# Pairwise bilinear products in FP32 parts: whole-pair PSUM tiles for VectorE, and a different place for the two-part weight loads

## The chip, the cores and the metric

The kernel runs on one NeuronCore of a Trainium2 chip. The metric is the device time of one execution in microseconds (us). The time before is 750.67 us, the median of three runs (748.7 to 752.8). One further execution was taken by the hardware profiler; all profile lines come from it.

## The reference

There are 32 fields of 128 numbers for each of 1024 rows of the batch, and one 128x128 matrix for each of the 496 pairs of fields i < j. Each pair's result is field i times its matrix, multiplied element by element with field j.

```python
FIELD_SIZE, EMBED_SIZE = 32, 128
_pairs = np.array(list(itertools.combinations(range(FIELD_SIZE), 2)), dtype=np.int32)   # 496 pairs
v_i = inputs[:, I_IDX, :]            # inputs: (1024, 32, 128) fp32
v_j = inputs[:, J_IDX, :]
transformed = jnp.einsum('bpd,ped->bpe', v_i, W)      # W: (496, 128, 128) fp32
return transformed * v_j             # (1024, 496, 128) fp32, 260 MB
```

## The kernel before, in words

**Layout.** Everything is held transposed: the 128 embedding positions lie on the partitions and the 1024 batch rows along them. The host only permutes inputs and outputs. Pairs are walked from i = 30 down to i = 0, and for each i over j = i+1 to 31, so a later field has more pairs (31 - i). A pair q is worked in two halves h of 512 batch rows; the loop counter u = 2q + h counts halves, 992 in all.

**Arithmetic.** The first 15 pairs (five fields, `NATIVE`) use plain FP32 matmuls (L209). All others split operands into parts that TensorE multiplies in its faster FP32R form. A matrix W becomes wh (ScalarE, L127), wl and wd (GpSimd, L128 to L130), two pairs at a time (`split_w`; 241 such chunks). A field x becomes xh (ScalarE, L142), xl (GpSimd, L143 and L144) and xd, half by half (`split_x`). For 16 fields xd is made on VectorE (L265), for the ten last ones on GpSimd (L148).

**One half.** `first(u)` takes a PSUM buffer, adds up the products wh·xh and wl·xl (L212), and ScalarE multiplies the sum in place by 1 + 2^-12 (L213). `second(u)`, called three halves later (`LAG = 3`), adds the third product wd·xd (L221). Then VectorE multiplies the PSUM buffer with field j into an output tile (L227). A PSUM buffer is 128x512, one bank; there are eight.

**Output.** Four pairs share an output tile of 2 MB, which is stored by one DMA from ScalarE's queue (L258) once all of it is written. There are seven such tiles at first. Four of them lie where groups of x fields are loaded later (L108, at the pairs of `XAT`), so that from pair 293 on only three are left.

**Weights.** W arrives in blocks of eight pairs, 512 KB, into three slots (`rpool`, `WB = 3`). Most blocks come by one DMA on SyncE's queue (L118). From block 12 on, every second one (`WAPART`) comes in two parts: 112 of the 128 rows by a DMA that GpSimd issues (L102), the other 16 by SyncE (L103). `back` notes that a few pairs later a tiny DMA of GpSimd's follows (`move_on`, L99). When each load is issued stands in a table `w_at`: for block c it is mostly pair 8c - 17. Near the end field 0 is loaded into one of the three W slots (`load_x(0)`).

**Order.** The order of instructions on each engine is that of the program text (`manual_schedule`); each engine works through its own list and waits where it needs another's result. W and x splits stand in `todo` with the earliest pair and the due pair; one of them is issued for each pair, the one due first. The GpSimd list is therefore a sequence of W chunks, with x halves put in wherever no chunk is ready.

Of the kernel before, what the change touches and what calls it, by code (L numbers as in the profile page):

```python
# [7 lines left out]
F32 = mybir.dt.float32  # L8
F32R = mybir.dt.float32r
ALU = mybir.AluOpType  # L10

P = 128
NF = 32
NQ = NF * (NF - 1) // 2
BT = 1024
HB = 512
WC = 2
WL = 8
OG = 4
EPS = 2.0**-12  # L20
NATIVE = 5
SHARED = 16
XDLAG = 10
LAG = 3
WB = 3
WLEAD = 12
XAFTER = 54
# [3 lines left out]
NE = 14  # L31
ROWS = 8 * NE
WAPART = tuple(range(12, 62, 2))
BACK = 3
XAT = (313, 219, 141, 52)
OWAIT = 20
SLAG = 2


def _pairs():  # L40
# [5 lines left out]
def kernel(  # L46
# [22 lines left out]
    nc = tc.nc  # L69
# [4 lines left out]
    spool = ctx.enter_context(tc.tile_pool(name="xs", bufs=2))  # L74
    rpool = ctx.enter_context(tc.tile_pool(name="wr", bufs=WB))
    wpool = ctx.enter_context(tc.tile_pool(name="ws", bufs=4))
    opool = ctx.enter_context(tc.tile_pool(name="o", bufs=1))
    ppool = ctx.enter_context(tc.tile_pool(name="ps", bufs=8, space=bass.MemoryType.PSUM))

    x_sb = {}  # L80

    def load_x(f, pieces=1, eng=None):
        if f == 0:

            t = rpool.tile([P, WL, P], F32, tag="w", name="x_0").rearrange("p q e -> p (q e)")
        else:
            t = xpool.tile([P, BT], F32, tag=f"x{f}", name=f"x_{f}")
        s = BT // pieces
        for k in range(pieces):
            (eng or nc.sync).dma_start(out=t[:, k * s : (k + 1) * s], in_=xt[f, :, k * s : (k + 1) * s])  # L90
        x_sb[f] = t

    w_raw = {}
# [3 lines left out]
    def move_on(k):  # L97

        nc.gpsimd.dma_start(out=mark[: 2 * k], in_=xt[0, : 2 * k, :16].rearrange("(b a) n -> a b n", a=k))  # L99

    def load_apart(dst, src):
        nc.gpsimd.dma_start(out=dst[:ROWS], in_=src[:ROWS].rearrange("(b a) m n -> a b m n", a=NE))  # L102
        nc.sync.dma_start(out=dst[ROWS:], in_=src[ROWS:])  # L103

    def load_group(k):
        t = xpool.tile([P, XG, BT], F32, tag=f"g{k}", name=f"x_g{k}")
        f = XG * k + 1
        nc.sync.dma_start(out=t, in_=xt[f : f + XG].rearrange("m d b -> (m d b)").rearrange("(d m b) -> d m b", m=XG, b=BT))  # L108
        for m in range(XG):
            x_sb[f + m] = t[:, m, :]  # L110

    def load_w(c, splits=(0, WL), eng=nc.sync):
        w_raw[c] = rpool.tile([P, WL, P], F32, tag="w", name=f"w_{c}")
        if c in WAPART:
            load_apart(w_raw[c], wt[c])
            return
        for a, b in zip(splits, splits[1:]):
            eng.dma_start(out=w_raw[c][:, a:b, :], in_=wt[c, :, a:b, :])  # L118

    w_s = {}  # L120

    def split_w(c, u):

        k = c * WC % WL
        raw = w_raw[c * WC // WL][:, k : k + WC, :].rearrange("p q e -> p (q e)")
        h, l, d = [wpool.tile([P, WC * P], F32R, tag=t, name=f"{t}_{c}") for t in ("wh", "wl", "wd")]
        nc.scalar.mul(h, raw, 1.0 - 2.0**-13)  # L127
        nc.gpsimd.tensor_tensor(l, raw, h.bitcast(F32), ALU.subtract)  # L128
        nc.gpsimd.tensor_scalar(d, h.bitcast(F32), EPS, 1.0, ALU.mult, ALU.mult)  # L129
        nc.gpsimd.tensor_tensor(d, l.bitcast(F32), d.bitcast(F32), ALU.subtract)  # L130
        w_s[c] = (h, l, d)

    x_s = {}
    later = []

    def split_x(f, a, u):
# [8 lines left out]
        if f > NF - 2 - NATIVE - SHARED:  # L145
            later.append((min(u + XDLAG, 2 * first_q[f] + LAG - 1), d, h.bitcast(F32), l.bitcast(F32)))
        else:
# [9 lines left out]
    for c in range(c0, nchunk):  # L157
        todo.append(((c - 3) * WC + 1, max(c * WC, nq0), lambda u, c=c: split_w(c, u)))
# [16 lines left out]
    w_at = {}  # L175
    for c in range(WB, -(-NQ // WL)):
        free = (c - WB + 1) * WL if (c - WB) * WL < nq0 else 0
        early = 0 if XAFTER < c <= XAFTER + WB else WLEAD - 6
        w_at[max(c * WL - 3 * WC - 5 - early, free)] = c
    x_at = XAFTER * WL - 11  # L180
    assert x_at not in w_at and len(w_at) == NQ // WL - WB

    w_q = {c: q for q, c in w_at.items()}
    back = []

    ngroup = NF // XG // 2
    group_at = {q: k for k, q in enumerate(XAT)}
# [4 lines left out]
    def out_tile(g):  # L192
        t = min((t for t in used if (g + 1) * OG <= until.get(t, NQ + OG)), key=used.get)
        used[t] = g
        pool = xpool if t in until else opool
        return pool.tile([P, OG, BT], F32, tag=t, name=f"ot_{g}")

    ctx.enter_context(tc.manual_schedule())
    po, ots, stores = {}, {}, []


    def first(u):
        q, h = divmod(u, 2)
        i, c = pairs[q][0], q // WC
        r = slice(q % WC * P, (q % WC + 1) * P)
        s = slice(h * HB, (h + 1) * HB)
        po[u] = ppool.tile([P, HB], F32, tag="po", name=f"po_{u}")
        if q < nq0:
            nc.tensor.matmul(po[u], w_raw[q // WL][:, q % WL, :], x_sb[i][:, s], start=True, stop=True)  # L209
        else:  # L210
            for t in (0, 1):
                nc.tensor.matmul(po[u], w_s[c][t][:, r], x_s[i][t][:, s], start=t == 0, stop=t == 1)  # L212
            nc.scalar.mul(po[u], po[u], 1.0 + EPS)  # L213

    def second(u):
        q, h = divmod(u, 2)
        i, j = pairs[q]
        r = slice(q % WC * P, (q % WC + 1) * P)
        s = slice(h * HB, (h + 1) * HB)
        if q >= nq0:  # L220
            nc.tensor.matmul(  # L221
                po[u], w_s[q // WC][2][:, r], x_s[i][2][:, s], start=False, stop=True, skip_group_check=True
            )
        g, k = divmod(q, OG)
        if k == 0 and h == 0:
            ots[g] = out_tile(g)
        nc.vector.tensor_tensor(ots[g][:, k, s], po.pop(u), x_sb[j][:, s], ALU.mult)  # L227
        if q >= NQ - 2:
            stores.append((u + SLAG, out[g, :, k, s], ots[g][:, k, s]))
        elif g == 0 or q >= NQ - OG:  # L230
            if h == 1:
                stores.append((u + SLAG, out[g, :, k], ots[g][:, k]))
        elif k == OG - 1 and h == 1:
            stores.append((u + SLAG, out[g], ots[g]))

    for u in range(2 * NQ + LAG + SLAG):
        q = u // 2
        if u < 2 * NQ:
            i, j = pairs[q]
            if u % 2 == 0 and j == i + 1 and XG * ngroup < i - 2 - XLEAD:  # L240
                load_x(i - 2 - XLEAD)
            first(u)
            if u == 2 * nq0:
                move_on(5)
            if u % 2 == 0 and q in group_at:
                load_group(group_at[q])
            if u % 2 == 1 and q in w_at:
                load_w(w_at[q])
                if w_at[q] in WAPART:
                    back.append(q + BACK)  # L250
            if u % 2 == 0 and q in back:
                move_on(16 - NE if q < w_q[WAPART[-1]] else 13)
            if u == 2 * x_at + 1:
                load_x(0)
        if LAG <= u < 2 * NQ + LAG:
            second(u - LAG)
        while stores and stores[0][0] <= u - LAG:
            nc.scalar.dma_start(*stores.pop(0)[1:])  # L258
        if u % 2 == 1:
            ready = [t for t in todo if t[0] <= q]  # L260
            if ready:
                ready[0][2](u)
                todo.remove(ready[0])
        while later and later[0][0] <= u:
            nc.vector.tensor_tensor(*later.pop(0)[1:], ALU.subtract)  # L265
    assert not todo and not later and not stores
# [32 lines left out]
```

## Time and profile before

| what | us |
|---|---|
| median of three runs | 750.67 |
| the profiled execution, its own time | 750.21 |
| its span, first to last instruction | 748.4 |
| PE busy (2946 matmul records) | 699.0 |
| VectorE busy | 678.0 |
| ScalarE busy | 623.9 |
| GpSimd busy | 611.5 |
| bytes moved by DMA | 310 MB, mean 414 GB/s |

The time of an execution is a little over its span, since starting and ending lie outside. In the profile PE is TensorE's matmul and PEld its weight load, DVE is VectorE, ACT ScalarE, POOL GpSimd and SP SyncE. A name such as "L213 ACT po<-po" gives the line of the kernel, the engine, and what is written from what. "Idle before" tells how long the engine stood before such an instruction and who released it. The granted TensorE clock was 0.984 of full speed.

### The profile page before, as it was taken

The numbers are of one execution on the slowest core, as the hardware profiler recorded it, in microseconds if no ns is written. First come the engines' busy times: TensorE is split into PE (matmuls) and PEld (weight loads), VectorE is DVE, ScalarE is ACT, GpSimd is POOL, SyncE is SP. The second block draws the span as 40 slices with busy tenths as digits, with TensorE's granted clock in tenths as the row PEclk, the third lists the DMA queues.
The fourth block names the chain that finished last, engine by engine and source line by source line (L and its number), as shares of the span: only waits on it lengthen the run. The fifth ranks groups of instructions, "written<-read, shape, count | busy, mean of one in ns | idle before, by whom it ended". The sixth has DMA issues, their size and how long they took to land.

```text
span 748.4 us, 11064 instructions
## 1 busy us (share of the span) xinstructions
PE 699.0 (93%) x2946; PEld 556.2 (74%) x2946; DVE 678.0 (91%) x1024; ACT 623.9 (83%) x1256; POOL 611.5 (82%) x902
## 2 busy tenths in 40 slices
PE   7998999999999999979999989899999999989994
PEld 3576778778888877858778777678787787868883
DVE  4999999999999998969989978689899899979994
ACT  1398989889999989968889888689899798969993
POOL 1889999999999988886988878688888889787760
PEclk9999999999999999999999999899999999999998
DMA  9999999999999999999999999999999999999998
GB/s 347 423 427 426 430 427 430 425 425 408 430 428 425 423 421 426 425 423 427 421 432 419 421 421 392 422 409 395 417 414 427 388 391 391 425 401 394 417 428 352
DMA packets 32941, 310.06 MB, mean 414 GB/s; under 512 B 5104, under 2 KB 5232, under 8 KB 16752
## 3 DMA queue, kind: packets, MB, share of 16 engines
q10 hardware_dynamic: 19584, 261.10, 83.0%
q1 hardware_dynamic: 8864, 36.77, 12.3%
q0 software_dynamic: 4432, 11.48, 4.2%
q8 instruction: 24, 0.39, 0.2%
q14 instruction: 37, 0.30, 0.1%
HBM read 49.29 MB, written 260.05 MB: 413 GB/s over the span
## 4 chain that ended last, share of the span: by engine, by line
PE 65%; DMA 14%; POOL 11%; DVE 6%; issue 2%; ACT 0%; DVEq 0%; ACTq 0%; POOLq 0%; SPq 0%
PE po L212 41%; PE po L221 21%; DMA out_dram<-ot 9%; DVE ot L227 6%; PE po L209 4%; DMA x<-in_xt_dram 3%; POOL wl L128 3%; POOL xl L143 2%; POOL wd L130 2%; POOL xd L148 2%; DMA w<-in_wt_dram 1%; POOL xl L144 1%; POOL wd L129 1%; DVE xd L265 1%; ACT po L213 0%
## 5 line engine op out<-in xcount | busy, mean ns | idle before, releaser
L213 ACT ACTIVATE po<-po 128x512 f32<-128x512 f32 x962 | 544.1, 584 | 84.8 <-PE po L212 48.4
L227 DVE TENSOR_TENSOR ot<-po,x 128x512 f32<-128x512 f32 x720 | 473.8, 687 | 36.9 <-DMA out_dram<-ot 17.6
L212 PE MATMUL po<-xl,wl 128*128 128x512 f32 x962 | 380.2, 395 | 19.8 <-POOL wl L128 18.5
L212 PE MATMUL po<-xh,wh 128*128 128x512 f32 x962 | 379.1, 394 | 10.3 <-DVE ot L227 10.3
L221 PE MATMUL po<-xd,wd 128*128 128x512 f32 x962 | 377.9, 393 | 4.2 <-ACT po L213 2.4
L212 PEld LDWEIGHTS po<-xl,wl 128*128 128x128 f32 x962 | 182.5, 190 | 65.4 <-POOL wl L128 25.8
L128 POOL TENSOR_TENSOR wl<-w,wh 128x256 fp32r<-128x256 f32 x241 | 180.3, 748 | 56.5 <-ACT wh L127 51.7
L212 PEld LDWEIGHTS po<-xh,wh 128*128 128x128 f32 x962 | 182.4, 190 | 51.5 <-DVE ot L227 13.2
L221 PEld LDWEIGHTS po<-xd,wd 128*128 128x128 f32 x962 | 182.3, 190 | 44.0 <-issue 3.5
L227 DVE TENSOR_TENSOR ot<-po,x_g 128x512 f32<-128x512 f32 x272 | 179.9, 689 | 24.1 <-PE po L221 18.9
L130 POOL TENSOR_TENSOR wd<-wl,wd 128x256 fp32r<-128x256 f32 x241 | 179.4, 744 | 20.1
L129 POOL TENSOR_SCALAR wd<-wh 128x256 fp32r<-128x256 f32 x241 | 99.1, 411 | 20.6
L127 ACT ACTIVATE wh<-w 128x256 fp32r<-128x256 f32 x241 | 99.4, 413 | 14.0 <-DMA w<-in_wt_dram 8.9
L143 POOL TENSOR_TENSOR xl<-x_g,xh 128x512 fp32r<-128x512 f32 x32 | 41.5, 1296 | 0.1
L144 POOL TENSOR_SCALAR xl<-xl 128x512 fp32r<-128x512 f32 x52 | 36.2, 696 | 4.6
L143 POOL TENSOR_TENSOR xl<-x,xh 128x512 fp32r<-128x512 f32 x20 | 26.3, 1313 | 15.8 <-ACT xh L142 15.5
L209 PE MATMUL po<-x,w 128*128 128x512 f32 x60 | 28.3, 628 | 4.0 <-DMA x<-in_xt_dram 4.0
L265 DVE TENSOR_TENSOR xd<-xh,xl 128x512 fp32r<-128x512 f32 x32 | 29.8, 930 | 0.0
L148 POOL TENSOR_TENSOR xd<-xh,xl 128x512 fp32r<-128x512 f32 x20 | 25.7, 1286 | 1.7
L209 PEld LDWEIGHTS po<-x,w 128*128 128x128 f32 x60 | 11.6, 198 | 19.9 <-issue 12.2
L142 ACT ACTIVATE xh<-x 128x512 fp32r<-128x512 f32 x20 | 12.4, 629 | 11.5 <-DMA x<-in_xt_dram 11.4
L142 ACT ACTIVATE xh<-x_g 128x512 fp32r<-128x512 f32 x32 | 20.2, 631 | 0.0
(7 smaller groups left out, 33.8 us busy)
## 6 DMA issues: line engine op xcount, KB each, us to landing
out_dram<-ot ACTq DMA_DIRECT2D x122, 2048.0 KB, 13.3
w<-in_wt_dram SPq DMA_DIRECT2D x36, 512.0 KB, 11.1
w<-in_wt_dram POOLq DMA_DIRECT2D x25, 448.0 KB, 11.8
x_g<-in_xt_dram SPq DMA_DIRECT2D x4, 2048.0 KB, 20.2
x<-in_xt_dram SPq DMA_DIRECT2D x14, 512.0 KB, 8.9
out_dram<-ot ACTq DMA_DIRECT2D x6, 512.0 KB, 8.6
w<-in_wt_dram SPq DMA_DIRECT2D x26, 64.0 KB, 5.9
x<-in_xt_dram ACTq DMA_DIRECT2D x4, 256.0 KB, 5.9
```

The lines of the kernel that those rows point to most:

```text
L127: nc.scalar.mul(h, raw, 1.0 - 2.0**-13)
L128: nc.gpsimd.tensor_tensor(l, raw, h.bitcast(F32), ALU.subtract)
L129: nc.gpsimd.tensor_scalar(d, h.bitcast(F32), EPS, 1.0, ALU.mult, ALU.mult)
L130: nc.gpsimd.tensor_tensor(d, l.bitcast(F32), d.bitcast(F32), ALU.subtract)
L143: nc.gpsimd.tensor_tensor(l, x_sb[f][:, s], h.bitcast(F32), ALU.subtract)
L144: nc.gpsimd.tensor_scalar(l, l.bitcast(F32), 1.0 / EPS, 1.0, ALU.mult, ALU.mult)
L148: nc.gpsimd.tensor_tensor(d, h.bitcast(F32), l.bitcast(F32), ALU.subtract)
L209: nc.tensor.matmul(po[u], w_raw[q // WL][:, q % WL, :], x_sb[i][:, s], start=True, stop=True)
L212: nc.tensor.matmul(po[u], w_s[c][t][:, r], x_s[i][t][:, s], start=t == 0, stop=t == 1)
L213: nc.scalar.mul(po[u], po[u], 1.0 + EPS)
L221: nc.tensor.matmul(po[u], w_s[q // WC][2][:, r], x_s[i][2][:, s], start=False, stop=True, skip_group_check=True)
L227: nc.vector.tensor_tensor(ots[g][:, k, s], po.pop(u), x_sb[j][:, s], ALU.mult)
```

## The change

PSUM tiles are now 128x1024, two banks, one for each pair, and there are four (`PB`). The two halves of a pair are still multiplied and scaled one after the other, `LAG` is still 3, and each half still lies in one bank. VectorE multiplies when both halves are done: one instruction of 1024 elements in place of two of 512, except for the last two pairs. `apart` tells the framework that the named instructions need not wait for each other. The two-part loads leave the table `w_at`: such a load is issued as soon as the program has issued the last split of the block whose slot becomes free (`spent`). The tiny DMA follows three pairs after it, as before.

```diff
-    ppool = ctx.enter_context(tc.tile_pool(name="ps", bufs=8, space=bass.MemoryType.PSUM))
+    ppool = ctx.enter_context(tc.tile_pool(name="ps", bufs=PB, space=bass.MemoryType.PSUM))
...
+    scaled, taken, halved = {}, {}, {}
+
+    def apart(inst, other, reason="the halves of a pair lie in two banks"):
+        if other is not None:
+            tc.declare_no_dep(inst.ins, other.ins, reason=reason)
...
-        nc.scalar.mul(h, raw, 1.0 - 2.0**-13)
+        halved[c] = nc.scalar.mul(h, raw, 1.0 - 2.0**-13)
+        apart(halved[c], halved.get(c - 4), "one engine writes both, in order")
...
+        if (c + 1) * WC % WL == 0:
+            spent.append(c * WC // WL)
...
-        w_at[max(c * WL - 3 * WC - 5 - early, free)] = c
+        if c not in WAPART:
+            w_at[max(c * WL - 3 * WC - 5 - early, free)] = c
...
+    w_next = list(WAPART)
...
-        po[u] = ppool.tile([P, HB], F32, tag="po", name=f"po_{u}")
+        if h == 0:
+            po[q] = ppool.tile([P, BT], F32, tag="po", name=f"po_{q}")
...
             for t in (0, 1):
-                nc.tensor.matmul(po[u], w_s[c][t][:, r], x_s[i][t][:, s], start=t == 0, stop=t == 1)
-            nc.scalar.mul(po[u], po[u], 1.0 + EPS)
+                m = nc.tensor.matmul(po[q][:, s], w_s[c][t][:, r], x_s[i][t][:, s], start=t == 0, stop=t == 1)
+                apart(m, scaled.get(u - 1) if h else None)
+            scaled[u] = nc.scalar.mul(po[q][:, s], po[q][:, s], 1.0 + EPS)
+            apart(scaled[u], taken.get(q - PB), "TensorE's products, which this waits for, have waited for it")
...
-            nc.tensor.matmul(
-                po[u], w_s[q // WC][2][:, r], x_s[i][2][:, s], start=False, stop=True, skip_group_check=True
+            m = nc.tensor.matmul(
+                po[q][:, s], w_s[q // WC][2][:, r], x_s[i][2][:, s], start=False, stop=True, skip_group_check=True
             )
+            apart(m, scaled[u ^ 1])
...
-        nc.vector.tensor_tensor(ots[g][:, k, s], po.pop(u), x_sb[j][:, s], ALU.mult)
+        if q >= NQ - 2:
+            nc.vector.tensor_tensor(ots[g][:, k, s], po[q][:, s], x_sb[j][:, s], ALU.mult)
+        elif h == 1:
+            taken[q] = nc.vector.tensor_tensor(ots[g][:, k, :], po.pop(q), x_sb[j], ALU.mult)
...
             if u % 2 == 1 and q in w_at:
                 load_w(w_at[q])
-                if w_at[q] in WAPART:
-                    back.append(q + BACK)
...
+        if w_next and (XAFTER if w_next[0] == XAFTER + 2 else w_next[0] - WB) in spent:
+            load_w(w_next.pop(0))
+            back.append(q + BACK)
```

More of the change, by code (lines that the diff above doesn't have):

```diff
@@ L24 @@
 LAG = 3
+PB = 4
 WB = 3
@@ L37 @@
 SLAG = 2
+PB = 4
 def _pairs():
@@ L118, in load_w @@
             eng.dma_start(out=w_raw[c][:, a:b, :], in_=wt[c, :, a:b, :])
-    w_s = {}
+    scaled, taken, halved = {}, {}, {}
+    def apart(inst, other, reason="the halves of a pair lie in two banks"):
+        if other is not None:
+            tc.declare_no_dep(inst.ins, other.ins, reason=reason)
+    w_s, spent = {}, []
     def split_w(c, u):
@@ L178 @@
         early = 0 if XAFTER < c <= XAFTER + WB else WLEAD - 6
-        w_at[max(c * WL - 3 * WC - 5 - early, free)] = c
+        if c not in WAPART:
+            w_at[max(c * WL - 3 * WC - 5 - early, free)] = c
     x_at = XAFTER * WL - 11
-    assert x_at not in w_at and len(w_at) == NQ // WL - WB
-    w_q = {c: q for q, c in w_at.items()}
+    assert x_at not in w_at and len(w_at) == NQ // WL - WB - len(WAPART)
     back = []
+    w_next = list(WAPART)
     ngroup = NF // XG // 2
@@ L206, in first @@
         s = slice(h * HB, (h + 1) * HB)
-        po[u] = ppool.tile([P, HB], F32, tag="po", name=f"po_{u}")
+        if h == 0:
+            po[q] = ppool.tile([P, BT], F32, tag="po", name=f"po_{q}")
         if q < nq0:
-            nc.tensor.matmul(po[u], w_raw[q // WL][:, q % WL, :], x_sb[i][:, s], start=True, stop=True)
+            nc.tensor.matmul(po[q][:, s], w_raw[q // WL][:, q % WL, :], x_sb[i][:, s], start=True, stop=True)
         else:
             for t in (0, 1):
-                nc.tensor.matmul(po[u], w_s[c][t][:, r], x_s[i][t][:, s], start=t == 0, stop=t == 1)
-            nc.scalar.mul(po[u], po[u], 1.0 + EPS)
+                m = nc.tensor.matmul(po[q][:, s], w_s[c][t][:, r], x_s[i][t][:, s], start=t == 0, stop=t == 1)
+                apart(m, scaled.get(u - 1) if h else None)
+            scaled[u] = nc.scalar.mul(po[q][:, s], po[q][:, s], 1.0 + EPS)
+            apart(scaled[u], taken.get(q - PB), "TensorE's products, which this waits for, have waited for it")
     def second(u):
@@ L248 @@
                 load_w(w_at[q])
-                if w_at[q] in WAPART:
-                    back.append(q + BACK)
             if u % 2 == 0 and q in back:
-                move_on(16 - NE if q < w_q[WAPART[-1]] else 13)
+                move_on(16 - NE if w_next else 13)
             if u == 2 * x_at + 1:
```

## The prediction

> **What bounds the kernel now.** I read the transfer part of the page first, because every pair leaves 0.52 MB of output behind.
>
> ```profile
> DMA  9999999999999999999999999999999999999998
> q10 hardware_dynamic: 19584, 261.10, 83.0%
> q1 hardware_dynamic: 8864, 36.77, 12.3%
> q0 software_dynamic: 4432, 11.48, 4.2%
> ```
>
> The shares are of 16 DMA engines over the span. They add to 99.5% (99.8% with two small queues), so the engines hardly rest. But a packet counts as busy however slowly it goes, so I asked for busy times by stage. The columns are the stage, its length, busy us (and instructions) of PE, PEld, DVE, ACT and POOL, then clock, DMA share and GB/s.
>
> ```profile
> 200.00:345.00 145.00, 138.78 (x598) 112.49 (x597) 133.78 (x209) 127.13 (x259) 126.70 (x190) 0.99 1.01 424
> 345.00:485.00 140.00, 128.94 (x551) 104.35 (x551) 121.76 (x184) 118.06 (x238) 116.97 (x173) 0.98 1.01 419
> 485.00:600.00 115.00, 110.25 (x476) 90.17 (x475) 106.64 (x158) 101.63 (x204) 97.57 (x146) 0.98 0.99 409
> 600.00:740.00 140.00, 132.76 (x575) 108.19 (x573) 128.73 (x195) 120.86 (x241) 103.79 (x159) 0.99 1.00 408
> ```
>
> The share stays full while the rate falls from 424 to 408 GB/s: late in the kernel the engines are not fed quite as fast as they could drain. The waits of VectorE show the same border.
>
> ```profile
> DVE ot L227 <- DMA out_dram<-ot: 20.2, 11, 5.2
> ```
> ```profile
> 479.28 4.41 DVE L227 TENSOR_TENSOR ot<-po,x 128x512 f32<-128x512 f32 x7 [5.18 <-DMA out_dram<-ot]
> ```
>
> The columns of the first are us in total, times and longest; the second is VectorE's timeline. VectorE waits 20.2 us in all for an output tile to be stored, the longest at 479 us; after 485.7 us only 1.8 us of it is left. The median store lands after 16.3 us between 200 and 440 us, after 9.8 us between 485 and 740 us. So up to about 485 us **transfers** set the pace and compute has some 18 to 20 us to spare; from there to 737 us **TensorE** sets it, and its idle time counts nearly one for one.
>
> In that last stage TensorE idles six times:
>
> ```profile
> 503.36 0.50 PE L212 MATMUL po<-xl,wl 128*128 128x512 f32 x1 [1.16 <-POOL wl L128]
> ...
> 540.81 0.50 PE L212 MATMUL po<-xl,wl 128*128 128x512 f32 x1 [1.78 <-POOL wl L128]
> ...
> 667.90 0.47 PE L221 MATMUL po<-xd,wd 128*128 128x512 f32 x1 [1.64 <-ACT po L213]
> ```
>
> The other three, also behind GpSimd's wl, are 1.80 at 581, 1.16 at 622 and 1.79 at 662 us: 9.3 us in all. GpSimd's timeline explains the two sizes. When it prepares the next field's x it runs x half, W split, x half, W split without a break. A burst that holds one DMA issue (0.62 us on L102, 0.63 on L99) ends in 1.78, one without in 1.16. The stall at 668 is a late load:
>
> ```profile
> 648.24 0.33 SPq L103 DMA_DIRECT2D w<-in_wt_dram  x1
> 655.54 0.62 POOL L102 DMA_DIRECT2D w<-in_wt_dram  x1
> 666.85 0.42 ACT L127 ACTIVATE wh<-w 128x256 fp32r<-128x256 f32 x1 [6.18 <-DMA w<-in_wt_dram]
> ```
>
> SyncE's 16 rows of block 56 leave at 648.24, GpSimd's 112 rows 7.3 us later, stuck in a burst, and ScalarE then stands 6.18 us.
>
> **What the Trainium skill says.** "VectorE: DVE Perf Modes", section on the TRN2 errata, gives an fp32 tensor_tensor as (N+151)/0.96 ns: 691 for N=512, where the trace has 687 and 689, so I use it for N=1024. "PSUM — Partial Sum Buffer", section on bank collisions, says different engines may work in different banks together; the trace agrees in that TensorE writes one half while VectorE reads another with both at full pace. "DMA: Bandwidth & Descriptors", section "Issuing engines are not separate DMA queues", says all queues interleave on the same 16 engines; 99.8% agrees, so an earlier load reorders traffic and adds no bandwidth.
>
> **The change part by part.** Steady pace first: two pairs (one W chunk) take 2.72 us, by the start of wh from one chunk to the next. That is twelve matmuls 0.227 apart.
>
> 1. *VectorE.* 988 half products become 494 pair products; four halves stay at the end. Eight halves in 4.87 us (row at 325 us) give (4.87 - 0.687)/7 = 0.598 each. A pair costs 0.598 + 512/0.96 = 1.131 (duration estimated at 1.224). Saved: 494 x (1.196 - 1.131) = 32 us of VectorE. Worth nothing by itself: VectorE needs 2.39 of each 2.72 us now, and it waits for TensorE or for stores.
>
> 2. *The PSUM ring.* Eight half buffers become four pairs; same banks, but both are freed together. With S = 0.681 us per half on TensorE, a half's buffer is now free for four S = 2.72 between its third product and its next first product. A pair has three S = 2.04 from the third product of its second half. Into these go 0.16 until that matmul ends, 0.04 to wake VectorE, 1.22 and 0.05 back, and 0.22 because the weight load carries the wait: 1.69, so 0.35 to spare. Nothing in steady state. What no longer hides is L265: 32 xd of 930 ns on VectorE, about 0.85 extra each, all of them started before 299 us. TensorE may lose 0.85 - 0.35 = 0.5 each, 16 us in all (bounds 0, if POOL and x waits coincide with them, and 27, if nothing is absorbed). This lies where compute has 18 to 20 us to spare, so I count zero on the end; without that cover it would be the 16.
>
> 3. *ScalarE.* The listing of waits has a new one: the second half's L213 waits for ScalarE's own first half. Today consecutive L213 overlap: with input ready they start 0.493 apart though each lasts 0.584. A wait for the predecessor makes it 0.584 + 0.03 (wake-up as after TensorE) = 0.62, 0.13 more for two of four. No row shows it on ScalarE; GpSimd's L130 waits for GpSimd itself and starts 0.08 after its predecessor, where unwaited ones start 0.04 before: 0.12. Bounds 0.10 and 0.20. ScalarE's chunk goes from 2.28 to 2.54 of 2.72. Two xh of 0.52 per field still fit where a field has 12 pairs or more; the shorter ones lose under 2 us, early, hidden as in 2. Dropped waits on wh were long satisfied: zero.
>
> 4. *Loads.* SyncE's 16 rows don't move: its queue already waits for the slot (253.8 us in 25 waits), and one x group load changes place with one of them, nothing behind it being due. GpSimd's part moves 5 to 11 us forward, directly behind the split that frees the slot, where GpSimd idles 0.67 per chunk against 0.62. By the listing of GpSimd's order the bursts change so. At 503: none, as before. At 541: loses its issue, -0.62. At 581 and 662: lose a load, but a mark issue now stands right before them, 0. At 622: gains one, +0.62. The stall at 668 goes: block 56 leaves about 6 us sooner, -1.64.
>
>    What is late next is block 57. The slots rotate differently: it used the slot of x_0, free at 659.5, and now gets block 55's, free at 664.3, and SyncE asks for it behind 58's rows. With 11 us to land it is there at 675.5, and ScalarE wants it near 673. A wait of 2.6 costs TensorE about 0.9 (at 668, 6.18 cost 1.64 beside 1.79 already lost). Bounds 0 and 3, since late loads land in 8 to 12 us. Queued behind it are ScalarE's L213 and the stores.
>
> 5. *Third product three halves later:* LAG is 3 in both; nothing moves.
>
> Sum for the last stage: -0.62 + 0.62 - 1.64 + 0.9 = -0.7 us. The profiled execution took 750.2 (span 748.4), 0.5 under the median, so I take 0.7 from the median: **about 750.0**.
>
> **Rivals.**
> *A, faster.* Block 57 arrives in time and marks fall into GpSimd's idle 0.67, so 581 and 662 drop to 1.16 too: -0.62 x 3 + 0.62 - 1.64 = -2.9, and a transfer queue that never runs dry gains a microsecond or more: 746. If all six stalls went, 741. For it: 668 us is a plain late issue. Against: the bursts stay.
> *B, slower.* The PSUM ring makes TensorE pay for each xd. It decides once the loss passes 20 us / 32 = 0.62 per xd; at 0.85 it is 27 - 20 = 7 over, 757.5. For it: xd rows up to 1.59 us. Against: an xd often falls where TensorE waits anyway.
> *C, slower.* The self-wait costs ScalarE more than 0.22, whereupon it is the slowest engine; at 0.30 a chunk takes 2.88, and 88 chunks of the last stage add 14: 764. Against: GpSimd's 0.12.
> *D, nothing moves*, since transfers bound more of the end than I think: 750.7.
>
> **How the numbers follow.** A measurement of this kernel can tell about 0.5% from no change: 3.75 us, so 746.9 to 754.4 is "same". Forecast 0.44 and D 0.10 lie in it. A 0.23, around 746: 0.21 of it under 746.9, 0.02 within. B 0.15 and C 0.08: over 754.4. Faster 0.21, same 0.56, slower 0.23. The range leaves out the worst of C and of A's full gain: 743.5 to 758.
>
> **What would show it.** Right: pair products of about 1.22 us, VectorE's busy time down from 678 to about 635 (494 x 1.224 + 32 x 0.93); no ScalarE wait for block 56; one of 1 to 4 us for block 57 near 670; waits for stored tiles before 485 us smaller than 20.2; four bursts still stalling at 1.2 to 1.8. Wrong: TensorE waiting for VectorE or ScalarE in the steady chunks after 485 us, a chunk over 2.75, or VectorE never waiting for stores (the early cover was used up).

## The result and the profile after

| | before | after |
|---|---|---|
| median of 20 runs, us | 750.02 (746.14 to 755.51) | 752.91 (750.42 to 755.32) |
| ratio after/before, 95% interval | | 1.0038 [1.0022, 1.0054] |
| span of the profiled execution, us | 748.4 | 752.9 |
| last matmul ends at, us | 737.3 | 745.0 |
| VectorE busy, us | 678.0 | 628.6 |

The change costs 2.9 us where I had forecast a gain of 0.7. That is under 0.5%, but the interval leaves out 1. A lower clock of TensorE is not the reason: the mean granted clock of the 20 executions after was 0.988, and the kernel before has 0.983 to 0.985 on the four chips of the experiments. Ratios leave out two slow executions, one of 2478 us of the kernel in which VectorE reads halves and one of 759.8 us of the kernel before. The profiled execution lost 4.5 us of span, more than the median did, so its differences show where time went and the ratios say how much. The time from the last matmul to the end shrank from 11.0 to 7.9 us, so the 7.7 us that TensorE lost count only in part.

These are the DMA rows of the page of the kernel after: busy share and rate in 40 slices, then the queue of the stores.

```profile
DMA  9999999999999999999999999999999999999988
GB/s 345 423 428 427 428 429 426 430 403 379 411 411 423 426 424 426 423 426 418 422 432 422 425 425 402 424 393 392 422 411 424 396 420 401 416 413 405 420 361 338
q10 hardware_dynamic: 19584, 261.10, 82.6%
```

The bytes are those of before, and nearly so the share (82.6 for 83.0%). The rate is not: the ninth to the twelfth slice (151 to 226 us, 18.8 us each) read 403, 379, 411 and 411, where before had 425, 408, 430 and 428. The 87 GB/s that the four lack together are worth 87 x 18.8 / 425 = 3.8 us of moving. The busy row, all nines there, hides this.

Next the busy times by stage of the kernel after; the columns are those that the prediction explained. The second fence is the first stage of the kernel before, which the prediction did not show.

```profile
50.00:200.00 150.00, 142.27 (x599) 112.20 (x599) 136.46 (x118) 134.58 (x268) 136.47 (x193) 0.99 1.00 418
200.00:345.00 145.00, 141.91 (x615) 114.45 (x614) 132.89 (x113) 134.72 (x268) 130.30 (x192) 1.00 1.01 421
345.00:485.00 140.00, 127.56 (x550) 102.51 (x549) 111.56 (x92) 120.09 (x238) 118.84 (x177) 1.00 1.01 421
485.00:600.00 115.00, 110.00 (x469) 88.06 (x469) 93.76 (x79) 101.59 (x202) 95.79 (x143) 0.99 1.00 409
600.00:740.00 140.00, 134.79 (x579) 107.27 (x579) 115.76 (x97) 123.91 (x243) 104.77 (x161) 1.00 0.98 403
```
```profile
50.00:200.00 150.00, 142.35 (x616) 114.55 (x615) 148.64 (x225) 134.82 (x275) 138.18 (x196) 1.00 1.01 426
```

The first stage is the one that I had left out. By 200 us the kernel after has done 17 matmuls fewer in the same stretch (599 against 616), and the rate fell from 426 to 418 GB/s: 8 x 150 / 425 = 2.8 us of transfers. In the last stage the rate is 403 against 408. In this execution stores hold up the last stage too: after 485 us VectorE waits 18 times for a stored tile, 17.1 us in all (before: 3 times, 1.8), and TensorE stands 4.9 us behind VectorE's pair products, a sign that the prediction had named as wrong. Before, it never did so there. Two more traces of the same code (the two runs without the waits at the end, below) have one such wait each, of 4.0 and 3.8 us near 490 us, and none later.

The waits of the kernel after: total us, times, longest us. Then the two of before that answer to its first two lines.

```profile
PEld po L226 <- DVE ot L247: 32.2, 44, 3.8
PE po L226 <- DVE ot L247: 14.1, 17, 3.4
DVE ot L247 <- DMA out_dram<-ot: 25.9, 22, 4.2
PE po L237 <- DVE ot L245: 2.4, 2, 1.2
ACT wh L136 <- DMA w<-in_wt_dram: 2.0, 1, 2.0
ACT po L228 <- ACT po L228: 1.0, 4, 0.3
```
```profile
PEld po L212 <- DVE ot L227: 13.2, 7, 3.7
PE po L212 <- DVE ot L227: 10.3, 6, 3.3
```

Four things are to be seen. TensorE's weight loads for a first product now wait for VectorE 44 times instead of 7; many of these waits pass while earlier matmuls still run, and the matmuls themselves stand 14.1 us instead of 10.3. A wait that did not exist before stops TensorE twice, behind the half products of the last two pairs (L245). ScalarE's wait for a late block is 2.0 us, at block 57. And ScalarE's wait for itself, which I feared for the steady pace, comes to 1.0 us in this list. The list leaves out waits under 0.15 us; the trace has 290 more, of 0.03 us each.

### The profile page after: what moved, and what is told of

Read it like the earlier page. It is cut to its first block, busy times and chain, and to the rows that moved or that the text cites. A ratio compares the mean times of both kernels' runs of the same rounds, so it can differ in the third digit from the quotient of the medians.

```text
span 752.9 us, 10606 instructions
## 1 busy us (share of the span) xinstructions
PE 705.0 (94%) x2946; PEld 551.4 (73%) x2946; DVE 628.6 (83%) x530; ACT 636.3 (85%) x1256; POOL 613.4 (81%) x902
## 3 DMA queue, kind: packets, MB, share of 16 engines
q10 hardware_dynamic: 19584, 261.10, 82.6%
## 4 chain that ended last, share of the span: by engine, by line
PE 58%; POOL 13%; DMA 13%; DVE 8%; issue 4%; ACT 2%; ACTq 0%; SPq 0%; DVEq 0%; POOLq 0%
PE po L226 37%; PE po L237 18%; DMA out_dram<-ot 10%; DVE ot L247 5%; PE po L223 3%; POOL xl L155 3%; POOL wl L138 3%; POOL xd L160 3%; DMA x_g<-in_xt_dram 2%; DVE xd L286 2%; POOL wd L140 2%; POOL xl L156 1%; ACT po L228 1%; POOL wd L139 1%; DMA x<-in_xt_dram 1%
## 5 line engine op out<-in xcount | busy, mean ns | idle before, releaser
L228 ACT ACTIVATE po<-po 128x512 f32<-128x512 f32 x962 | 554.2, 584 | 81.6 <-PE po L226 66.9
L247 DVE TENSOR_TENSOR ot<-po,x 128x1024 f32<-128x1024 f32 x358 | 432.4, 1222 | 78.3 <-DMA out_dram<-ot 18.3
L226 PE MATMUL po<-xh,wh 128*128 128x512 f32 x962 | 381.0, 396 | 15.5 <-DVE ot L247 14.1
L237 PE MATMUL po<-xd,wd 128*128 128x512 f32 x962 | 377.1, 392 | 6.7 <-ACT po L228 3.1
L226 PEld LDWEIGHTS po<-xh,wh 128*128 128x128 f32 x962 | 181.3, 189 | 69.2 <-DVE ot L247 32.2
L138 POOL TENSOR_TENSOR wl<-w,wh 128x256 fp32r<-128x256 f32 x241 | 183.4, 761 | 57.3 <-ACT wh L136 53.1
L237 PEld LDWEIGHTS po<-xd,wd 128*128 128x128 f32 x962 | 181.3, 189 | 47.5 <-ACT po L228 4.8
L247 DVE TENSOR_TENSOR ot<-po,x_g 128x1024 f32<-128x1024 f32 x136 | 164.9, 1224 | 37.0 <-PE po L237 15.6
L286 DVE TENSOR_TENSOR xd<-xh,xl 128x512 fp32r<-128x512 f32 x32 | 33.7, 1054 | 0.3 <-POOL xl L156 0.3
```

What stands on the lines that cost most here:

```text
L226: m = nc.tensor.matmul(po[q][:, s], w_s[c][t][:, r], x_s[i][t][:, s], start=t == 0, stop=t == 1)
L228: scaled[u] = nc.scalar.mul(po[q][:, s], po[q][:, s], 1.0 + EPS)
L237: m = nc.tensor.matmul(po[q][:, s], w_s[q // WC][2][:, r], x_s[i][2][:, s], start=False, stop=True, skip_group_check=True)
L247: taken[q] = nc.vector.tensor_tensor(ots[g][:, k, :], po.pop(q), x_sb[j], ALU.mult)
```

## Where the time went

**Behind each xd on VectorE.** The first fence is VectorE's timeline of the kernel after around one xd, the second TensorE's.

```profile
224.34 1.46 DVE L286 TENSOR_TENSOR xd<-xh,xl 128x512 fp32r<-128x512 f32 x1
225.72 2.34 DVE L247 TENSOR_TENSOR ot<-po,x 128x1024 f32<-128x1024 f32 x2
```
```profile
226.99 0.50 PE L226 MATMUL po<-xh,wh 128*128 128x512 f32 x1 [0.43 <-DVE ot L247]
```

VectorE makes xd for 1.46 us, then reads two pairs without a pause. TensorE's next first product needs the buffer pair that the first of them frees, and stands 0.43 us. Other such places cost 0.4 to 0.7 us each. From 205 to 255 us TensorE's matmuls lose about 2.6 us this way; before, 0.1. The mechanism and the size of one stall are those of the prediction's step 2 (0.5 each). The sum is not. In those traces of the experiments below in which no half clock (see below) falls into the stretch, TensorE starts 1028 matmuls between 50 and 300 us with pair products and the new loads, and 1033 to 1038 with half products (three traces); with the old loads it is 1030 and 1036 with pairs against 1045 before. At 0.227 us each, the 5 to 15 matmuls are 1.1 to 3.4 us, not 16: where TensorE stands behind VectorE, another wait often falls away. Behind GpSimd's wl, for one, it stands 3.0 us there with pairs and 5.9 with halves.

**Why it is not hidden.** The median time from issue to landing of the stores issued between 150 and 200 us says how much is queued; this is the row of the kernel after, then of before.

```profile
out_dram<-ot ACTq DMA_DIRECT2D x9, 2048.0 KB, 8.9
```
```profile
out_dram<-ot ACTq DMA_DIRECT2D x9, 2048.0 KB, 11.4
```

Between 200 and 440 us the same figure was 16.3 us before; at 150 to 200 us it was 11.4, so there was less to lend. The 8.9 of the kernel after is not the ring's doing alone. Here are TensorE's timeline and the busy times of one stretch, first after, then before.

```profile
160.02 0.71 PE L226 MATMUL po<-xl,wl 128*128 128x512 f32 x1 [2.02 <-POOL wl L138]
```
```profile
160.00:171.00 11.00, 10.98 (x41) 8.94 (x42) 7.79 (x7) 8.11 (x16) 8.84 (x15) 0.84 0.90 375
```
```profile
157.41 0.51 PE L212 MATMUL po<-xl,wl 128*128 128x512 f32 x1 [0.87 <-POOL wl L128]
```
```profile
160.00:171.00 11.00, 11.00 (x51) 9.10 (x50) 11.00 (x17) 10.56 (x22) 10.21 (x16) 1.00 1.01 422
```

TensorE first waits 2.02 us for GpSimd, where it waited 0.87 before. That comes with the loads: the kernel with the new loads alone has such a wait of 1.93 us, the pairs with the old loads have none over 0.3 us between 50 and 300 us. Then, from 160.1 to 163.6 us, TensorE's clock is halved (0.84 on average over the row), and matmuls start 0.43 us apart instead of 0.23, which costs 1.6 us more. Wait and half clock make 2.8 of the 3.9 us that the 17 matmuls missing at 200 us are worth.

A trace of the same code without that half clock (the first run without the waits at the end) has 423 GB/s in the first stage and a landing time of 9.7 us. The kernel in which VectorE reads halves has 423 GB/s and 9.9 us, and it loses no time. So this stretch shows how little could be hidden early. It does not show that the ring's loss became time here; where that happened stays open.

**At the end.** TensorE's timeline of the kernel after:

```profile
742.29 0.74 PE L237 MATMUL po<-xd,wd 128*128 128x512 f32 x2 [1.24 <-DVE ot L245]
744.17 0.79 PE L237 MATMUL po<-xd,wd 128*128 128x512 f32 x1 [1.14 <-DVE ot L245]
```

In the last two pairs VectorE still multiplies half by half. Both halves now lie in one tile, so the third product of the second half (L237) waits until VectorE has read the first half (L245), although they share no byte. Before, the halves were two tiles. No other multiplication is left to cover this: 2.4 us.

## The experiments

Every ratio is to the kernel before, over five rounds on the same chip, with its 95% interval. Not all experiments were on one chip, and a difference of two ratios carries both intervals. Four theories stood against each other: the **ring** (Theory 1: a pair freed as a whole makes TensorE pay for VectorE's xd early on), the **tail** (the two waits for L245), the **self-wait** of ScalarE, and the **loads**.

### The loads alone, and the pairs alone

The first is the kernel before with only the new place of the two-part loads:

```diff
-        w_at[max(c * WL - 3 * WC - 5 - early, free)] = c
+        if c not in WAPART:
+            w_at[max(c * WL - 3 * WC - 5 - early, free)] = c
...
+        if w_next and (XAFTER if w_next[0] == XAFTER + 2 else w_next[0] - WB) in spent:
+            load_w(w_next.pop(0))
+            back.append(q + BACK)
```

> The kernel before with the new place of the two-part loads alone; half-size PSUM buffers and half products as before. Theory 1 (the pair ring costs the time: each xd on VectorE stops TensorE, and the cover around 160 us was thin): ratio to before 0.995 to 1.001; no stall of TensorE behind VectorE around each xd, last matmul near 736 us. Theory 2 (the new place of the loads costs it, since load and tiny DMA now fall into early x bursts of GpSimd): ratio 1.003 or more, with a TensorE stall of about 2 us at 160 us and transfers running dry there.

Measured: 0.9998 [0.9982, 1.0014]. The second is the kernel after with those lines taken back:

> The changed kernel with the two-part loads put back to their old places; whole-pair PSUM tiles and pair products kept. Theory 1 (pair ring): ratio to before 1.003 to 1.006, TensorE stalls of 0.4 to 0.7 us behind VectorE at each xd remain, and ScalarE waits some 6 us for block 56 near 668 us. Theory 2 (loads): ratio 0.998 to 1.001.

Measured: 1.0026 [1.0008, 1.0044]. The loads neither gain nor lose anything that can be told; the loss comes with the pairs. In the trace of the first, two effects of the loads stand against each other: the stall that Theory 2 named is there (1.93 us behind GpSimd's wl at 142 us, then half clock from 143.5 to 146.9), and ScalarE's late wait for a block is gone.

### Without the waits at the end

The kernel after, in which the second half's third product is declared apart from the first half's L245:

```diff
+            apart(m, ends.get(u - 1) if h else None)
...
-            nc.vector.tensor_tensor(ots[g][:, k, s], po[q][:, s], x_sb[j][:, s], ALU.mult)
+            ends[u] = nc.vector.tensor_tensor(ots[g][:, k, s], po[q][:, s], x_sb[j][:, s], ALU.mult)
```

> The changed kernel; the third product of a second half no longer waits for VectorE's product of the first half in the last two pairs (they lie in different banks). Theory 3 (part of the loss is at the very end, two stalls of TensorE of 1.2 us each): last matmul 2.4 us earlier and the time 1.5 to 2.4 us lower, ratio to before about 1.001. Theory 1 alone: the stores are still queued at the end, so under 0.7 us lower, ratio 1.003 to 1.004.

Measured: 1.0005 [0.998, 1.0029]. The same kernel again, since the interval is wide:

> The changed kernel without the two waits at the end once more, to narrow the interval and to compare with ten such waits on the same chip. Theory 3: 1.000 to 1.002. Theory 1 alone: 1.003 to 1.004.

Measured: 1.0025 [1.0005, 1.0044]; the mean of the two is 1.0015, which lies between the two expectations. The same edit with the loads in their old place:

> The changed kernel with the two-part loads at their old places and without the two waits at the end: pair tiles and pair products alone. Theory 3 (the two stalls at the end make most of the loss): 1.5 to 2.4 us below the same kernel with the two waits, ratio to before 0.999 to 1.001. Theory 1 (pair ring and xd) without 3: ratio stays 1.002 to 1.003.

Measured: 1.0015 [0.9998, 1.0032], again between the two. Against their partners that have the waits this is 1.0038 - 1.0015 = 0.23% and 1.0026 - 1.0015 = 0.11%.

### Pair tiles, but VectorE reads halves

The edit above, and L247 taken out: every half is multiplied by itself, as before. The pair tiles, `apart` and ScalarE's self-wait stay.

> The changed kernel with pair tiles, but VectorE multiplies halves again, each as soon as its third product is done; no third product waits for VectorE. After the last third product VectorE then needs 0.69 instead of 1.22 us before a pair's banks come free, so 0.88 instead of 0.35 us to spare. Theory 1: the stalls behind xd nearly vanish, ratio to before 0.996 to 1.001. If what costs the time is elsewhere (ScalarE's wait for itself, the loads): ratio stays 1.002 or more, less 2.4 us at the end, which e3 tells.

Measured: 0.9993 [0.9965, 1.002]. Its waits, one row of the list:

```profile
PEld po L226 <- DVE ot L245: 15.9, 14, 4.0
```

14 waits in place of 44, near the 7 of before: a VectorE instruction of one half gives TensorE back its cover. ScalarE's self-wait is in this kernel and costs nothing that can be told. Once more:

> Pair tiles with VectorE multiplying halves, no third product waiting for VectorE, once more beside the kernel without the two waits at the end. Theory 1 in its small form (what the ring leaves of the loss is 0.5 to 1 us): 0.0005 to 0.0015 lower than that kernel. Without it: no lower.

Measured: 1.0001 [0.9981, 1.0021]. And with the two waits at the end put back (the `apart` of L245 only for earlier pairs):

> Pair tiles with VectorE multiplying halves (which measured 0.9993 and 1.0001), and the two waits of TensorE for VectorE put back in the last two pairs alone. If the two waits make 1.5 us or more of the loss: ratio to before 1.0015 to 1.003, last matmul 2 us later than without them. If they are hidden behind queued stores: 0.999 to 1.001.

Measured: 1.0015 [1.0000, 1.0031], 0.18% over the mean 0.9997 of the two without. TensorE stood 0.85 and 1.15 us at the end. So the tail is put back by itself, and costs 0.1 to 0.2% in three comparisons, 0.17% or 1.3 us on average. With the intervals of the ratios taken as independent, that average is good to 0.13 points: 0.04 to 0.31%.

### xd in two pieces

The kernel without the waits at the end, with each xd on VectorE cut into two of 256 elements, issued two halves apart (the first one two halves earlier than a whole xd):

```diff
-            later.append((min(u + XDLAG, 2 * first_q[f] + LAG - 1), d, h.bitcast(F32), l.bitcast(F32)))
+            for k in (0, 1):
+                p = slice(k * HB // 2, (k + 1) * HB // 2)
+                due = min(u + XDLAG + 2 * k - 2, 2 * first_q[f] + LAG - 1)
+                later.append((due, d[:, p], h[:, p].bitcast(F32), l[:, p].bitcast(F32)))
```

> The changed kernel without the two waits at the end, and each xd cut into two pieces of 256 elements, a half counter apart, so that none holds VectorE longer than about 0.45 us. Theory 1: the stalls behind xd go, ratio to before 0.997 to 1.000, below that of the kernel with whole xd (1.0005). Theory 3 alone: same as with whole xd, 1.000 to 1.001.

Measured: 1.0000 [0.9979, 1.0021]. The pair products remain, what stands between two of them is smaller, and the rest of the loss is gone as far as the interval tells. The stalls shrink but do not go: between 50 and 300 us TensorE's matmuls stand 2.1 us behind VectorE's products, against 3.3 to 5.4 with whole xd (the three traces without the waits at the end) and 0.3 to 1.3 with half products (three traces). The mean of the three kernels with whole xd, pair products and no wait at the end is 1.0015; that of the three that take one or the other away (this one and the two of halves) is 0.9998. The difference puts the ring at 0.17%, 1.3 us, and reckoned as above it is good to 0.18 points. These ratios alone do not quite tell it from nothing; the doubled xd of the next section tells more.

### xd made twice

To weigh the suspected cost, each xd on VectorE is computed twice, with the same values. First in the kernel before:

```diff
+            nc.vector.tensor_tensor(*later[0][1:], ALU.subtract)
```

> The kernel before with every xd on VectorE computed twice in a row (the second writes the same values again): 32 times about 0.85 us more on VectorE. With half-size buffers there are about 2 us to spare before TensorE notices, so both theories expect few stalls behind VectorE and a ratio to before of 0.999 to 1.004.

Measured: 1.0164 [1.0122, 1.0206], a clear miss. The added rows take 28 us of VectorE (25.7 and 32.2 in place of 29.8), nearly all before 300 us, and 0.0164 x 750 = 12 us reach the end. The 2 us to spare were too many in the prediction's own terms: for a half they are 2.72 - (0.16 + 0.04 + 0.69 + 0.05 + 0.22) = 1.56, and two xd in a row hold VectorE 1.8 us. The profiled execution took 767.9 us, 6.3 over the median, at a clock of 0.974, so what follows from its trace shows where and not how much. Of TensorE's waits, those for xd itself grow by 5.3 us (7.1 against 1.8), those for a PSUM buffer by 6.0 (16.3 against 10.3). The rate row of its page:

```profile
GB/s 343 426 411 409 313 423 417 364 430 398 388 400 426 420 431 422 425 416 426 428 426 423 423 413 407 417 405 356 416 422 423 388 393 389 432 377 376 406 430 349
```

The slices at 77 to 96 us (313) and 134 to 153 us (364) show transfers that had run out of work (all 16 engines together stood about 3.6 us between 78 and 82 us; TensorE had run at half clock from 75.0 to 78.4), long before the waits that I had counted as cover even began, at 295 us. Next the same line in the kernel after:

> The changed kernel with every xd on VectorE computed twice in a row. Theory 1 (the pair ring has only 0.35 us to spare): each doubled xd costs TensorE its whole 0.85 us more, 27 us until 300 us, of which the queue of stores can hide 10 to 18: ratio to before 1.012 to 1.025. Theory 3 (the end alone): no more than the same doubling adds to the kernel before, ratio 1.003 to 1.008.

Measured: 1.0296 [1.0261, 1.0332]. Doubling adds 1.0296 - 1.0038 = 2.58 points here and 1.64 there. The difference, 0.94 points (good to 0.57) or 7 us, is 0.22 us for each of the 32. TensorE's waits say why: those for xd grow by 4.5 us, much as in the kernel before, but those for a PSUM buffer by 17.3 (31.4 against 14.1) where halves gave 6.0. Pairs make each microsecond that VectorE spends elsewhere dearer.

### Ten pairs at the end by halves

The kernel after with half products, and so with the wait for L245, in the last ten pairs:

```diff
-        if q >= NQ - 2:
+        if q >= NQ - 10:
```

> The changed kernel with VectorE's half products, and with them the wait of each second half's third product for VectorE, in the last ten pairs in place of the last two. Theory 3 (a wait at the end counts in full once the queue of stores has run short): eight more stalls of 1.2 us, 9.8 us of TensorE, of which stores still queued hide 2 to 4: ratio to before 1.010 to 1.018. If the end is hidden behind the stores in any case: ratio stays 1.003 to 1.006.

Measured: 1.0052 [1.003, 1.0074], only 0.14% over the kernel after: a miss. TensorE's timeline:

```profile
739.71 0.49 PE L237 MATMUL po<-xd,wd 128*128 128x512 f32 x1 [0.39 <-DVE ot L245]
741.75 0.50 PE L237 MATMUL po<-xd,wd 128*128 128x512 f32 x1 [0.38 <-DVE ot L245]
743.80 0.50 PE L237 MATMUL po<-xd,wd 128*128 128x512 f32 x1 [0.39 <-DVE ot L245]
745.85 0.73 PE L237 MATMUL po<-xd,wd 128*128 128x512 f32 x2 [0.85 <-DVE ot L245]
747.73 0.51 PE L237 MATMUL po<-xd,wd 128*128 128x512 f32 x1 [1.15 <-DVE ot L245]
```

Eight stalls of 0.4 us (five of them before these lines) are added to the two of 0.85 and 1.15, not eight of 1.2. These eight are 3.1 us of TensorE, and the ratio is 1 us over that of the kernel after; for the original two the comparisons above give 1.3 us of 2.4. So a part of such a stall seems to be hidden even at the end, by my reading behind stores that queue anyway. The first difference is good only to 0.27 points, so how large a part is not shown.

### xd of all fields on VectorE

A version suggested by the runs: since the bursts on GpSimd were what stalled TensorE late, the last ten fields' xd go to VectorE too, in the kernel before with the new place of the loads.

```diff
-SHARED = 16
+SHARED = 26
```

> A try for a faster version: the kernel before with the new place of the loads, and xd of the ten last fields on VectorE too (SHARED = 26). GpSimd's bursts get shorter by two times 1.29 us, so TensorE's stalls of 1.2 to 1.8 us behind wl in the last stage should go, 7 to 9 us of TensorE; transfers bound what that is worth: ratio to before 0.993 to 0.998. If VectorE's longer list costs as much: 0.999 to 1.003.

Measured: 0.9938 [0.9917, 0.996], 746.77 us: faster than both kernels. The same with the old loads:

> The kernel before with xd of all fields on VectorE (SHARED = 26), loads at their old places. Half-size buffers leave 2 us before TensorE notices an xd: as with the new place of the loads (0.9938), ratio 0.992 to 0.997. If the gain needed the new place of the loads: 0.998 or more.

Measured: 0.9984 [0.9967, 1.0001]. In both, TensorE's stalls behind wl after 485 us, 7.7 us before, are gone. The clearest difference lies at one place. With the old loads (ScalarE's timeline, then TensorE's):

```profile
664.12 0.42 ACT L127 ACTIVATE wh<-w 128x256 fp32r<-128x256 f32 x1 [5.62 <-DMA w<-in_wt_dram]
```
```profile
665.16 0.77 PE L221 MATMUL po<-xd,wd 128*128 128x512 f32 x1 [4.57 <-ACT po L213]
```

With the new loads the longest such wait of ScalarE, and TensorE after it:

```profile
671.80 0.42 ACT L127 ACTIVATE wh<-w 128x256 fp32r<-128x256 f32 x1 [2.16 <-DMA w<-in_wt_dram]
```
```profile
672.85 0.47 PE L224 MATMUL po<-xd,wd 128*128 128x512 f32 x1 [0.32 <-ACT po L216]
```

Block 56 comes late with the old loads, and TensorE, which no burst of GpSimd has held up shortly ahead of it, now pays 4.57 us where before it paid 1.64. From 664.5 to 671.3 us its clock is halved besides, which is worth some 3 us more. With the new loads 0.32 is left, without a half clock. The kernels differ by 3.4 us (0.9984 - 0.9938 = 0.46%). That is one execution of each; the other stalls differ as well, so the place is shown and the full amount is not. And with the pairs and no waits at the end:

> The changed kernel without the two waits at the end, and xd of all fields on VectorE. Theory 1 (pair ring): twenty more xd, each 0.4 to 0.7 us of TensorE, take back 8 to 10 us of the 7 to 9 that the shorter bursts of GpSimd give, as far as TensorE bounds the last stage: ratio to before 0.997 to 1.003, over that of e14. If the ring costs nothing: equal to e14.

Measured: 0.9987 [0.9966, 1.0008], the same as the kernel with halves and the old loads on this chip (0.9984), and 0.5% over the one with halves and the same new loads (on another chip). So pairs give up most of what moving xd with the new loads won. In the traces, after 485 us, TensorE stands behind VectorE's products 11 times, 7.1 us in all, where the halves with the same loads have 7 times, 4.2 us. The expectation had 8 to 10 us.

## The prediction, point by point

- **What bounds the kernel.** Right for the stages shown, wrong by leaving out the one from 50 to 200 us. The step that failed is in part 2: "This lies where compute has 18 to 20 us to spare, so I count zero on the end". The waits that make up these 20 us begin at 295 us, the longest stands at 479. They show that compute was ahead of the stores then. They lend nothing to 160 us, where the landing time was 11.4 us, as the trace of before could have said. The doubled xd shows it in the kernel before itself: 28 us of added early work on VectorE cost 12.
- **1, VectorE.** Sizes right: 1.222 and 1.224 us for a pair (estimated 1.224), busy time 628.6 (635). Two rows, the groups of the kernel after:

```profile
L247 DVE TENSOR_TENSOR ot<-po,x 128x1024 f32<-128x1024 f32 x358 | 432.4, 1222 | 78.3 <-DMA out_dram<-ot 18.3
L286 DVE TENSOR_TENSOR xd<-xh,xl 128x512 fp32r<-128x512 f32 x32 | 33.7, 1054 | 0.3 <-POOL xl L156 0.3
```

  The first row's idle 78.3 us is where the time saved went: VectorE waits for stores and for TensorE. The other failed step stands here: "four halves stay at the end" was counted at nothing. The two waits behind them cost about 1.3 us. A dependency that the change adds was read off for ScalarE, but not for TensorE.
- **2, the ring.** One stall is sized right, 0.4 to 0.7 us against 0.5; the sum and the cover are wrong. By the counts of matmuls TensorE loses 1.1 to 3.4 us in all and not 16, which is the reason given for the lower bound (other waits coincide). And about 1.3 us, not 0, reach the end. That it was rival B in small, far under its point of decision of 0.62 us each beyond all cover, shows that such a point is the wrong form: the loss is not all or nothing.
- **3, ScalarE.** Right. Where a second half waits for the first, they start about 0.62 us apart (0.62), and the kernel of pair tiles with half products shows no cost. Rival C falls.
- **4, the loads.** The waits went as said: block 56's is gone, block 57's is 1.99 us (2.6) and costs TensorE 0.68 (0.9), and four stalls behind wl of 0.81 to 1.16 and one of 0.33 are left after 485 us. They are short because TensorE had just stood behind VectorE in that execution: the same code in the first run without the waits at the end has 1.06, 1.25, 1.86, 1.86 and 1.87, where part 4 comes to 1.16, 1.16, 1.80, 1.78 and 1.79. Two things were left out. Before 485 us the load lengthens the wait at 160 us, from 0.87 to 2.02. And in the trace of before a half clock of 3.4 us follows the stalls at 581 and at 662 us, so that each cost about 1.6 us more than its own length. A sum of -0.7 us can't be told from the measured 0.9998. Rival A falls: block 57 does come late, and the bursts stay. So does D, by the interval.
- **5, LAG.** Nothing moved.

The sum that measures out is: tail +1.3, ring +1.3, loads 0, self-wait 0, together 2.6 of 2.9 us. That the two together are the loss is shown by the kernels that have neither (0.9993 and 1.0001). The tail's interval leaves out zero (0.04 to 0.31%). The ring's just includes it (0 to 0.35%); that pairs make xd on VectorE dearer is told by the doubled xd. Their exact shares stay open.

## What to carry to other kernels

Cover is a matter of time, not of sum: look at a queue's landing time in the very stretch where work gets slower, and do not count waits that come later. Look at the granted clock of that stretch too, before a difference between two traces is put down to the change. Joining two buffers into one joins their releases and their waits, so list for every engine, not just the one that gets slower, which instruction now waits for the other half, above all at the end, where nothing follows. A faster engine that already waits brings nothing; here, taking 25.7 us of xd off the engine whose bursts stalled TensorE, and moving the loads so that no late block took the bursts' place, did.

## What the runs showed of the hardware

- ScalarE's in-place multiplications of 584 ns start 0.493 us apart when nothing holds them, and about 0.62 (0.608 to 0.634) when each waits for the one before.
- One VectorE instruction read 1024 elements across two PSUM banks in 1.222 us, at a pitch of 1.13 to 1.14, with TensorE writing other banks beside it.
- xd on VectorE took 930 ns on average before and 1054 with pairs, there the shortest 684 and the longest 1636. No run here says why.
- In the stages of before and after the DMA busy share stood at 98 to 101% while the rate went from 426 down to 403 GB/s. The rate and the landing times (16.3, 11.4 and 8.9 us in the stretches above) moved where the share did not.
- TensorE's granted clock was either full or half, in stretches of 3.41 us or a multiple. Between 40 and 735 us of the 17 traces a half clock began 56 times. Each time TensorE had stood idle for 1.77 us or more of the 3.41 us just before, at once or in pieces. Of the stretches after a full clock none with less idle time was followed by a half clock; between 1.77 and 1.84 us both occur. So a wait of 2 us can cost 1.6 us on top of its own length, and it does not when it falls across the border of two stretches: the wait at 160 us was followed by a half clock at 2.02 us in one trace and not at 1.97 in another.
- Executions of one kernel scatter with that clock. Of the 59 of the kernel before beside the last three runs, the fastest (746.8 us) had a mean clock of 0.986, the slowest (756.6 us) of 0.974.
